# Two stacked graph-attention layers: the order of dense pieces, sums and transposes in the last stage

## The chip, the cores and the metric

The kernel runs on one core of a Trainium2 chip. The metric is the time of one execution on the device in microseconds. The kernel before took 2142.76 us, the median of three runs (2141.24 to 2143.43). Besides those there is one execution under the hardware profiler, which has a time of its own.

The engines named below are TensorE (PE in the profile; its weight loads are PEld), VectorE (DVE), ScalarE (ACT), GpSimd (POOL) and the synchronous engine that issues plain transfers (SP). SBUF is the on-chip memory, PSUM the accumulators that TensorE writes.

## The reference

There are 4096 nodes with 512 features each and one 0/1 adjacency matrix, sparse and densest at the low node numbers. `heads` is a graph-attention layer: the features are projected, each edge gets a leaky-ReLU score from its two ends, the scores of a node's edges go through a softmax, and the neighbours' projected rows are summed with these weights.

```python
x  = layernorm(x + heads(x, adj, W0, a0))                # layer 0: 8 heads of 64
h  = elu(heads(x, adj, W1, a1))                          # layer 1: 8 heads of 64
o  = elu(heads(h, adj, Wo, ao))                          # one head of 512
y  = relu(o @ lin1_w + lin1_b) @ lin2_w + lin2_b         # 512 -> 1024 -> 512
x  = layernorm(x + y)
```

All arithmetic is in float32. The change concerns the last three lines: the attention with one head of 512, the two dense layers behind it, and the residual and layernorm at the end.

## The kernel before, in words

**Stages.** The kernel first turns the adjacency into edge lists, with the projection for the first attention beside it; then come three attention stages. Each stage's projected rows lie in a table in device memory, from which the next one gathers. A last branch, for inputs whose lists would not fit, does not run here.

**Tiles, chunks, units.** The 4096 nodes are 32 tiles of 128. A tile's edges lie in chunks of 128, one edge to a partition. A unit is up to six chunks of one tile (`GC`); the last stage has 66 of them. Tiles 20 to 31 have one unit, tiles 5 to 19 two, tiles 1 to 4 three or four, and tile 0, the densest, has eleven in four parts.

**What a unit needs** (class `Attention`):
- `gather` (L1072): one indirect transfer for each chunk, issued by GpSimd, into one of four row buffers `g` (`GT`, so a buffer comes free when the sums of the unit four before are done).
- `spread` (L1085), once for each tile: small matmuls into `pss` put the destination's part of the score beside each edge; VectorE collects them (L1117, L1129). More than 20 chunks take several cuts, each collected before the next (L1121 to L1124).
- `weights` (L1135): three VectorE operations on the scores `z` (L1147 to L1150), and ScalarE's exponential `w` (L1158).
- `add` (L1160): VectorE makes weighted selection matrices `sm` from the node numbers and `w` (L1187), and TensorE multiplies them with the gathered rows into the tile's accumulator `acc` (L1212). These matmuls are called *sums* below.

**What a finished tile needs.** `inverse` (L1216) takes the reciprocal of the softmax's denominator, on VectorE. `fold` (L1437) divides (L1239, VectorE) and applies the ELU: two ScalarE operations (L1247, L1248) and one of VectorE (L1249). `turn` (L1442) transposes the result on TensorE (L1452) and lets ScalarE copy it from PSUM (L1453) into the block's buffer `sht`.

**Dense pieces.** Tiles come in nine blocks: 31, 30; then 29 to 26; then 1, 10, 11, 20; then 23, 0, 24, 25; then 2, 9, 12, 19; 3, 8, 13, 18; 4, 7, 14, 17; 5, 6, 15, 16; and 22, 21. When the last tile of a block is turned, the block's work for the two dense layers enters the list `ready` as pieces: as many of the first layer as the block has tiles (`first_dense`, L1468: matmuls L1475, ReLU by ScalarE L1478), then one of the second layer for each tile (`second_dense`, L1480). A second-layer piece loads the tile's residual row by SP (L1483), adds the bias to it on VectorE (L1484), and multiplies (L1487). Its epilogue stays in `open_` until `close` (L1464) is called: the sum with the residual (L1492), the layernorm (L1253 to L1266 on VectorE with two ScalarE operations, L1258 and L1259, between) and the store by SP (L1494). Residual rows have three buffers `xr`.

**What sets the order.** The stage is written under a manual schedule: every engine carries out its own instructions in the order in which the program issues them. The loop over the units (L1512 to L1533) is therefore the plan. A running number `due` grows by the unit's chunks times a `pace`, chosen so that a block's pieces are spread over the units of the next block; when it reaches one and `ready` isn't empty, a piece is issued. In the kernel before one pass of the loop issues, in this order: the score matmuls of a later tile; the transposes of the tile folded in the pass before; the weights of the next unit; the reciprocal of the tile just finished; the unit's `sm` and sums; a gather; the open epilogue; the fold of the tile just finished; the collection of the scores; and last the pieces that are due. After the loop come the last two turns and all the pieces that are left (L1534 to L1540).

Of the kernel before, what the change touches and what calls it, by code (L numbers as in the profile page):

```python
# [10 lines left out]
F32 = mybir.dt.float32  # L11
# [10 lines left out]
P = 128  # L22
N = 4096
F = 512
# [534 lines left out]
def sparse_path(  # L559
# [23 lines left out]
    nc = tc.nc  # L583
# [57 lines left out]
    x1_d = dram.tile([N, F], F32, name="sx1_d")  # L641
# [407 lines left out]
    def units_of(order):  # L1049
        units = []  # L1050
        for t in order:
            own = [
                Unit(t, [(p.first + i, n) for i, n in runs], slots)
                for p in pts if p.t == t for runs, *slots in p.units()
            ]
            own[0].first = own[-1].last = True
            units += own
        return units
# [186 lines left out]
    def elu(sb, o):  # L1245
        ex = sb.tile([P, F], F32, name="ex")
        nc.scalar.activation(ex, o, AF.Relu, scale=-1.0)  # L1247
        nc.scalar.activation(ex, ex, AF.Exp, scale=-1.0)  # L1248
        return lambda: nc.vector.scalar_tensor_tensor(o, ex, -1.0, o, op0=OP.add, op1=OP.max)  # L1249

    def layernorm(sb, y):
        bs = sb.tile([P, 6], F32, name="bs")
        nc.vector.bn_stats(bs, y)  # L1253
        mv = sb.tile([P, 2], F32, name="mv")
        nc.vector.bn_aggr(mv, bs)
        rs = sb.tile([P, 2], F32, name="rstd")
        lg, r = rs[:, 0:1], rs[:, 1:2]
        nc.scalar.activation(lg, mv[:, 1:2], AF.Ln, bias=eps)  # L1258
        nc.scalar.activation(r, lg, AF.Exp, scale=-0.5)  # L1259

        def rest():

            nc.vector.scalar_tensor_tensor(lg, mv[:, 1:2], EPS, r, op0=OP.add, op1=OP.mult)
            nc.vector.scalar_tensor_tensor(lg, lg, -0.5, r, op0=OP.mult, op1=OP.mult)
            nc.vector.scalar_tensor_tensor(r, lg, 1.5, r, op0=OP.add, op1=OP.mult)
            nc.vector.tensor_scalar(y, y, mv[:, 0:1], r, op0=OP.subtract, op1=OP.mult)  # L1266

        return rest
# [87 lines left out]
    with ExitStack() as pools:  # L1356
        big = pools.enter_context(tc.tile_pool(name="eb", bufs=1))
        sb = pools.enter_context(tc.tile_pool(name="es", bufs=2))
# [24 lines left out]
    sb = ctx.enter_context(tc.tile_pool(name="ls", bufs=2, reuse_waits="tile"))  # L1383
# [23 lines left out]
    with tc.tile_pool(name="tg", bufs=GT, side="right", reuse_waits="tile") as gp, \  # L1407
            tc.tile_pool(name="tb", bufs=1, side="right", reuse_waits="tile") as big, \
            tc.tile_pool(name="ta", bufs=2, space=PSUM, reuse_waits="tile") as pacc, \
            tc.tile_pool(name="tp", bufs=1, space=PSUM, reuse_waits="tile") as ps, tc.manual_schedule():  # L1410

        few = NT - 12
        blocks = [[NT - 1, NT - 2], [NT - 3 - i for i in range(NJ)]]
        blocks += [[1 + b, few // 2 - b, few // 2 + 1 + b, few - b] for b in range(few // NJ)]
        blocks.insert(3, [NT - 9, 0, NT - 8, NT - 7])
        blocks.append([NT - 10, NT - 11])
        assert sorted(sum(blocks, [])) == list(range(NT))
        order = [t for block in blocks for t in block]  # L1420
        units = units_of(order)
        at = Attention(st2, gp, wk, pacc, ps)
        for _ in range(GT):
            nc.gpsimd.memset(gp.tile([P, GC, F + HS], F32, name="g"), 0.0)
        for u in units[:GT]:
            at.gather(u)
        l1w = big.tile([P, FC, HID], F32, name="sl1w")
        nc.sync.dma_start(l1w, lin1_w.rearrange("(c p) o -> p c o", p=P))
        l2w = big.tile([P, HC, F], F32, name="sl2w")
        nc.sync.dma_start(l2w, lin2_w.rearrange("(c p) o -> p c o", p=P))  # L1430
        l1b_r = big.tile([HC, P], F32, name="sl1b_r")
        nc.sync.dma_start(l1b_r, lin1_b.rearrange("(c p) -> c p", p=P))
        l2b = big.tile([P, F], F32, name="sl2b")
        nc.sync.dma_start(l2b, lin2_b.partition_broadcast(P))
        hts, hids, ready, open_ = {}, {}, [], []

        def fold(t):  # L1437
            o = at.normal(sb, t)
            elu(sb, o)()
            return o  # L1440

        def turn(t, o):  # L1442
            b = next(b for b, block in enumerate(blocks) if t in block)
            j, nb = blocks[b].index(t), len(blocks[b])
            if j == 0:

                while any(r[1] == b - 2 and r[0] is first_dense for r in ready):
                    piece()
                hts[b] = big.tile([P, FC, NB], F32, name="sht", bufs=2)
            pt = ps.tile([P, FC, P], F32, name="pt")  # L1450
            for c in range(FC):
                nc.tensor.transpose(pt[:, c, :], o[:, ts(c, P)], ident)  # L1452
            nc.scalar.copy(hts[b][:, :, ts(j, P)], pt)  # L1453
            if j == nb - 1:
                per = HC // nb
                ready.extend((first_dense, b, range(i * per, (i + 1) * per)) for i in range(nb))
                ready.extend((second_dense, b, i) for i in range(nb))

        def piece():
            close()  # L1460
            of, *what = ready.pop(0)
            of(*what)

        def close():  # L1464
            while open_:
                open_.pop(0)()

        def first_dense(b, ks):  # L1468
            if 0 in ks:
                hids[b] = big.tile([P, HC, NB], F32, name="shid")  # L1470
            for k in ks:
                n = len(blocks[b]) * P
                p1 = ps.tile([P, NB], F32, name="p1", tag="p", bufs=2)[:, :n]
                for c in range(FC):
                    nc.tensor.matmul(  # L1475
                        p1, l1w[:, c, ts(k, P)], hts[b][:, c, :n], start=(c == 0), stop=(c == FC - 1)
                    )
                nc.scalar.activation(hids[b][:, k, :n], p1, AF.Relu, bias=l1b[:, k : k + 1])  # L1478

        def second_dense(b, j):  # L1480
            t = blocks[b][j]
            xr = sb.tile([P, F], F32, name="xr", bufs=3)
            nc.sync.dma_start(xr, x1_d[ts(t, P), :])  # L1483
            nc.vector.tensor_add(xr, xr, l2b)  # L1484
            p2 = ps.tile([P, F], F32, name="p2", tag="p", bufs=2)
            for k in range(HC):
                nc.tensor.matmul(  # L1487
                    p2, hids[b][:, k, ts(j, P)], l2w[:, k, :], start=(k == 0), stop=(k == HC - 1)
                )

            def rest():
                nc.vector.tensor_add(xr, p2, xr)  # L1492
                layernorm(sb, xr)()
                nc.sync.dma_start(out[ts(t, P), :], xr)  # L1494

            open_.append(rest)

        for t in order[:2]:
            at.spread(t)()
        at.weights(units[0])  # L1500
        l1b = big.tile([P, HC], F32, name="sl1b")
        pb = ps.tile([P, HC], F32, name="pt")
        nc.tensor.transpose(pb, l1b_r, ident[:HC, :HC])
        nc.vector.tensor_copy(l1b, pb)


        pace = {t: 0.0 for t in blocks[0]}
        for last, block in zip(blocks, blocks[1:]):
            chunks = sum(u.n for u in units if u.t in block)
            pace.update((t, 2 * len(last) / chunks) for t in block)  # L1510
        due, folded = 0.0, None
        for i, u in enumerate(units):  # L1512
            pos = order.index(u.t)
            spread = at.spread(order[pos + 2]) if u.first and pos + 2 < NT else None
            if folded:
                turn(*folded)
                folded = None
            if i + 1 < len(units):
                at.weights(units[i + 1])
            if u.first and pos > 0:  # L1520
                at.inverse(sb, order[pos - 1])
            at.add(u)
            if i + GT < len(units):
                at.gather(units[i + GT])
            close()
            if u.first and pos > 0:
                folded = order[pos - 1], fold(order[pos - 1])
            if spread:
                spread()
            due = min(due + u.n * pace[u.t], 2.5)  # L1530
            while due >= 1 and ready:
                due -= 1
                piece()  # L1533
        if folded:  # L1534
            turn(*folded)
        at.inverse(sb, order[-1])
        turn(order[-1], fold(order[-1]))
        while ready:
            piece()
        close()  # L1540
# [56 lines left out]
```

## Time and profile before

| what | us |
|---|---|
| median of three runs | 2142.76 |
| the profiled execution | 2328.89 |
| its span, first to last instruction | 2326.7 |
| the last stage in it | about 1550 to 2326.7 |
| busy in the span: TensorE / VectorE / GpSimd / ScalarE | 1776.6 / 1328.1 / 1161.8 / 658.9 |
| in 1550 to 2327, idle ahead of the transposes (L1452) | 29.0 |
| in 1550 to 2327, idle ahead of the sums (L1212) | 42.7 |
| in 1550 to 2327, idle of VectorE ahead of the bias on the residual row (L1484) | 65.3 |

In a line of the groups the columns are: source line, engine, operation, what it writes and reads, the shapes, how often; after the first bar the busy time in us and the mean of one in ns; after the second the time that the engine sat idle just before such instructions, and what ended it. A line of the timeline has start and duration in us, engine, line, operation, operands and count, and in brackets the idle time before it with its releaser. Matmuls of float32 are counted twice there: a dense piece is 16 or 32 of them. A wait that the profile ascribes to "issue" has no releaser that it can see. The span of the profiled execution is longer than the runs' median, so durations are taken from it and are added up against its own time.

### The profile page before, as it was taken

Reading aid. Unit: us, or ns where it says so; the run is one execution under the profiler, and the core shown is the slowest. Engines: PE = TensorE matmul, PEld = TensorE weight load, DVE = VectorE, ACT = ScalarE, POOL = GpSimd, SP = SyncE. Lnnn points to the kernel's source line nnn. Section 1 sums busy time; section 2 is a strip of 40 time slices with the busy share of each in tenths; the row PEclk is TensorE's granted clock in tenths of the full one; section 3 lists DMA queues with packets and bytes.
Section 4 is the critical chain, followed back from the end, with each engine's and each line's share of the span. In section 5 each row is a group of like instructions: output and inputs, shape, how many; then the busy total and the mean of one; then the engine's idle time right before and its main releaser. Section 6 shows DMA issues by size and latency. Waiting matters only on the chain.

```text
span 2326.7 us, 29282 instructions
## 1 busy us (share of the span) xinstructions
PE 1776.6 (76%) x8987; PEld 1038.4 (45%) x8987; DVE 1328.1 (57%) x3920; ACT 658.9 (28%) x2311; POOL 1161.8 (50%) x1662
## 2 busy tenths in 40 slices
PE   4778776643987775754997767746999898998997
PEld 3555442212665543531665444424445444444444
DVE  6887776744998776733777655733243424334322
ACT  3446776650332211100433221101111111121121
POOL 5424444456556664627556665646355634444300
PEclk9989997866999896875999988877999999999999
DMA  6434665525667775625566665545354524335301
GB/s 222 141 115 159 224 256 207 210 80 163 201 209 219 212 209 144 174 60 145 154 159 170 175 182 145 158 128 143 87 150 131 170 81 148 101 110 151 93 16 52
DMA packets 132589, 351.94 MB, mean 151 GB/s; under 512 B 41922, under 2 KB 42954, under 8 KB 128454
## 3 DMA queue, kind: packets, MB, share of 16 engines
q0 software_dynamic: 74160, 206.25, 33.1%
q1 hardware_dynamic: 58262, 143.72, 17.5%
q8 instruction: 74, 1.21, 0.2%
q14 instruction: 93, 0.76, 0.1%
HBM read 347.31 MB, written 42.24 MB: 167 GB/s over the span
## 4 chain that ended last, share of the span: by engine, by line
PE 36%; DVE 12%; issue 9%; another core or an unknown queue 6%; DMA 3%; POOL 3%; ACT 2%; SPq 0%; DVEq 0%; POOLq 0%; ACTq 0%
PE acc L1212 13%; PE p L1475 9%; PE ph L697 6%; PE p L1487 5%; DVE g L1200 4%; POOL g L1076 3%; DMA g<-table_t,idx 2%; DMA xr<-sx_d 1%; PE pt L683 1%; DVE bs L1253 1%; DVE sm L1179 1%; DVE sm L1187 1%; DVE xr L1492 1%; DVE z L1147 1%
## 5 line engine op out<-in xcount | busy, mean ns | idle before, releaser
L1076 POOL DMA_INDIRECT g<-table_t,idx x927 | 937.4, 1011 | 720.1 <-PE acc L1212 352.9
L1212 PE MATMUL acc<-g,sm 128*64 128x260 f32 (+2 forms) x4068 | 619.9, 424 | 219.9 <-DVE g L1200 100.7
L1212 PEld LDWEIGHTS acc<-g,sm 128*64 128x64 f32 x4068 | 347.9, 150 | 462.7 <-issue 177.8
L697 PE MATMUL ph<-sw_t,xt 128*128 128x264 f32 (+1 forms) x1536 | 408.4, 415 | 82.1 <-ACT xt L686 46.3
L697 PEld LDWEIGHTS ph<-sw_t,xt 128*128 128x128 f32 x1536 | 303.4, 204 | 154.2 <-ACT xt L686 63.0
L1200 DVE TENSOR_TENSOR g<-g,wp 128x2048 f32<-128x2048 f32 (+3 forms) x132 | 349.1, 2645 | 22.8 <-ACT wp L1155 20.2
L884 DVE MAX8 cand<-key 128x8 f32<-128x353 f32 (+55 forms) x467 | 197.3, 449 | 77.7 <-PE key L878 77.1
L1475 PE MATMUL p<-sht,sl1w 128*128 128x512 f32 (+1 forms) x576 | 229.3, 553 | 2.2 <-issue 1.2
L1487 PE MATMUL p<-sl2w,shid 128*128 128x512 f32 x512 | 227.0, 598 | 0.0
L686 ACT ACTIVATE xt<-pt 128x128 f32<-128x128 f32 x384 | 101.1, 278 | 286.5 <-PE pt L683 132.3
L710 ACT COPY hrow<-ph 128x260 f32<-128x260 f32 (+2 forms) x194 | 71.1, 373 | 311.1 <-PE ph L697 146.2
L1475 PEld LDWEIGHTS p<-sht,sl1w 128*128 128x128 f32 x576 | 107.6, 191 | 114.0 <-issue 108.7
L1487 PEld LDWEIGHTS p<-sl2w,shid 128*128 128x128 f32 x512 | 95.4, 190 | 120.1 <-issue 119.3
L1249 DVE SCALAR_TENSOR_TENSOR o<-ex,o 128x512 f32<-128x512 f32 x64 | 44.4, 694 | 182.8 <-ACT ex L1248 145.1
L877 PE MATMUL key<-sg,s_identb 128*128 128x512 bf16 (+1 forms) x258 | 111.6, 434 | 15.4 <-DVE cand L884 10.1
L848 ACT ACTIVATE sg<-raw 128x4096 bf16<-128x4096 int32 (+1 forms) x39 | 116.9, 2998 | 6.6 <-DMA raw<-in_adj_dram 3.7
L1478 ACT ACTIVATE shid<-p,sl1b 128x512 f32<-128x512 f32 (+1 forms) x72 | 46.0, 639 | 249.5 <-PE p L1475 212.0
L878 PE MATMUL key<-frac,places 128*128 128x512 bf16 (+1 forms) x258 | 111.1, 431 | 2.7 <-POOL places L784 2.7
L1187 DVE TENSOR_SCALAR sm<-iota_n,nl,w 128x64 f32<-128x64 f32 x339 | 83.1, 328 | 31.9 <-ACT w L1158 31.1
L1147 DVE TENSOR_TENSOR z<-s,g 128x16 f32<-128x16 f32 (+9 forms) x291 | 43.6, 174 | 92.0 <-DMA g<-table_t,idx 83.7
L1117 DVE TENSOR_REDUCE s<-pss 128x48 f32<-128x144 f32 (+21 forms) x108 | 32.1, 298 | 102.3 <-remote 55.1
L686 ACT ACTIVATION_READ_ACCUMULATOR xt<-pt 128x1 f32 x384 | 79.7, 208 | 0.0
(185 smaller groups left out, 1811.3 us busy)
## 6 DMA issues: line engine op xcount, KB each, us to landing
raw<-in_adj_dram SPq DMA_DIRECT2D x31, 2048.0 KB
table_t<-hrow SPq DMA_DIRECT2D x64, 260.0 KB
xr<-in_x_dram SPq DMA_DIRECT2D x64, 256.0 KB
g<-table_t,idx POOLq DMA_INDIRECT x927
table_t<-hrow SPq DMA_DIRECT2D x32, 257.0 KB
sx_d<-o SPq DMA_DIRECT2D x32, 256.0 KB
xr<-sx_d SPq DMA_DIRECT2D x32, 256.0 KB
out_dram<-xr SPq DMA_DIRECT2D x32, 256.0 KB
```

The lines of the kernel that those rows point to most:

```text
L686: nc.scalar.activation(xt[:, c, :], pt[:, c, :], AF.Copy, accum_out=st.xparts[:, c, t : t + 1])
L697: nc.tensor.matmul(ph[:n], columns(c), st.w[:, c, j], start=(c == 0), stop=(c == FC - 1))
L848: nc.scalar.activation(sg[:, ts(i, w)], raw[:, ts(i, w)], AF.Sign)
L877: nc.tensor.matmul(out_, ident_b, sg[:, j:e], start=True, stop=False)
L878: nc.tensor.matmul(out_, places[:, w], frac[:, j - w * KW : e - w * KW], start=False, stop=True)
L884: nc.vector.max(out=cand[:, at : at + 8], in_=part)
L1076: nc.gpsimd.indirect_dma_start(out=u.g[:, k, : self.st.row], out_offset=None, in_=self.st.table[:, :], in_offset=bass.IndirectOffsetOnAxis ...
L1187: nc.vector.tensor_scalar(sm[:, at + i], of_g, node[k], u.w[:, k], op0=OP.is_equal, op1=OP.mult)
L1200: nc.vector.tensor_mul(body, body, wp[:, :, :, None].to_broadcast(body.shape))
L1212: nc.tensor.matmul(out_[g * HN : (g + 1) * HN], sm[:, slot], rows(k), start=start, stop=stop)
L1475: nc.tensor.matmul(p1, l1w[:, c, ts(k, P)], hts[b][:, c, :n], start=(c == 0), stop=(c == FC - 1))
L1487: nc.tensor.matmul(p2, hids[b][:, k, ts(j, P)], l2w[:, k, :], start=(k == 0), stop=(k == HC - 1))
```

## The change

Five edits, all in the last stage.

- The list `ready` is looked at right after a pass has issued the score matmuls: `due` is counted up there, and one piece is issued if one is due, ahead of the weights, the `sm` and the sums of the unit. Pieces beyond it are issued where they were, at the end of the pass.
- The transposes of the tile folded in the pass before are issued behind the unit's sums and gather and ahead of the open epilogue. Before, they stood ahead of the weights and the sums.
- `due` is no longer counted up at the end of the pass.
- The load of a residual row is a function of its own, `rows_of`, which loads a row at most once.
- `piece` calls it for the piece next in the list, if that is one of the second layer, before it issues the piece at hand; `second_dense` finds its row loaded, or loads it.

```diff
-        hts, hids, ready, open_ = {}, {}, [], []
+        hts, hids, resid, ready, open_ = {}, {}, {}, [], []
...
         def piece():
             close()
             of, *what = ready.pop(0)
+
+            if ready and ready[0][0] is second_dense:
+                rows_of(*ready[0][1:])
             of(*what)
+
+        def rows_of(b, j):
+            t = blocks[b][j]
+            if t not in resid:
+                resid[t] = sb.tile([P, F], F32, name="xr", bufs=3)
+                nc.sync.dma_start(resid[t], x1_d[ts(t, P), :])
...
         def second_dense(b, j):
             t = blocks[b][j]
-            xr = sb.tile([P, F], F32, name="xr", bufs=3)
-            nc.sync.dma_start(xr, x1_d[ts(t, P), :])
+            rows_of(b, j)
+            xr = resid.pop(t)
             nc.vector.tensor_add(xr, xr, l2b)
...
             spread = at.spread(order[pos + 2]) if u.first and pos + 2 < NT else None
-            if folded:
-                turn(*folded)
-                folded = None
+            due = min(due + u.n * pace[u.t], 2.5)
+            if due >= 1 and ready:
+
+                due -= 1
+                piece()
             if i + 1 < len(units):
                 at.weights(units[i + 1])
...
             if i + GT < len(units):
                 at.gather(units[i + GT])
+            if folded:
+                turn(*folded)
+                folded = None
             close()
...
             if spread:
                 spread()
-            due = min(due + u.n * pace[u.t], 2.5)
             while due >= 1 and ready:
```

## The prediction, made before the changed kernel was run

> **What bounds the kernel now.** I read first the page, to see which engine carries the span. All busy shares are averages over four stages, so I then took the groups of instructions of the last stage alone (1550 us to the end), because the change touches nothing before it:
>
> ```profile
> L1475 PE MATMUL p<-sht,sl1w 128*128 128x512 f32 (+1 forms) x576 | 229.3, 553 | 2.2 <-issue 1.2 <-DVE xr L1492 1.0
> L1487 PE MATMUL p<-sl2w,shid 128*128 128x512 f32 x512 | 227.0, 598 | 0.0
> L1212 PE MATMUL acc<-g,sm 128*64 128x257 f32 (+1 forms) x1356 | 204.7, 421 | 42.7 <-DMA g<-table_t,idx 23.2 <-DVE rd L1224 10.3 <-DVE sm L1187 4.8
> ...
> L1452 PE MATMUL pt<-s_ident,o 128*128 128x128 f32 x128 | 23.0, 310 | 29.0 <-DVE o L1249 16.2 <-issue 12.8
> ...
> L1484 DVE TENSOR_TENSOR xr<-xr,sl2b 128x512 f32<-128x512 f32 x32 | 22.1, 691 | 65.3 <-DMA xr<-sx_d 60.3 <-issue 5.0
> ```
>
> TensorE is busy for 680 of 777 us: the stage is its own work plus its gaps. So an edit pays only by closing a gap. The largest are 23.2 us at the start for the first gathers, which stay, and 29.0 us ahead of the transposes. VectorE loses 60.3 us on the residual rows, but VectorE has room. The third view is the timeline at a place where the transposes wait (tile 25 ends the fourth block, tile 2 begins the fifth):
>
> ```profile
> 1852.08 7.13 PE L1487 MATMUL p<-sl2w,shid 128*128 128x512 f32 x16
> ...
> 1859.75 3.13 PE L1212 MATMUL acc<-g,sm 128*64 128x257 f32 x24
> ...
> 1860.36 0.70 DVE L1492 TENSOR_TENSOR xr<-p,xr 128x512 f32<-128x512 f32 x1
> ...
> 1863.64 0.75 DVE L1239 TENSOR_SCALAR o<-acc,rd 128x512 f32<-128x512 f32 x1
> ...
> 1865.74 0.73 DVE L1249 SCALAR_TENSOR_TENSOR o<-ex,o 128x512 f32<-128x512 f32 x1 [1.36 <-ACT ex L1248]
> ...
> 1866.53 1.12 PE L1452 MATMUL pt<-s_ident,o 128*128 128x128 f32 x4 [3.65 <-DVE o L1249]
> ...
> 1867.26 1.42 DVE L1187 TENSOR_SCALAR sm<-iota_n,nl,w 128x64 f32<-128x64 f32 x6
> 1867.62 5.27 PE L1212 MATMUL acc<-g,sm 128*64 128x257 f32 x24
> ```
>
> Two things are to be seen. VectorE works in one order: end of the dense piece's epilogue, then the fold (L1239 to L1249), and only then the sm of the next unit (L1187). And the sums after the gap take 5.27 us where 24 of them elsewhere take 2.82.
>
> The last view is the timeline of TensorE where tile 20 ends the third block, the shape that matters most below:
>
> ```profile
> 1744.31 7.13 PE L1487 MATMUL p<-sl2w,shid 128*128 128x512 f32 x16
> ...
> 1751.39 0.63 PE L1452 MATMUL pt<-s_ident,o 128*128 128x128 f32 x4
> 1751.95 2.82 PE L1212 MATMUL acc<-g,sm 128*64 128x257 f32 x24
> 1754.70 7.13 PE L1475 MATMUL p<-sht,sl1w 128*128 128x512 f32 x16
> ```
>
> No gap at all: a dense piece of 7.1 us runs while VectorE folds and makes the next sm.
>
> [...]here 24 sums cost 5.27 against 2.82 us after 3.65 us idle, and 16 cost 3.77 against 1.95 after 2.42[...]. [...]the residual load at 1949.10 lets its add start at 1954.13, the last one at 2312.62 at 2316.39, so 3.8 to 5.0 us here.
>
> **The change, part by part.** I wrote out the loop's two orders through the 66 units; the old one gives the trace's order exactly. "Piece" is 7.1 us of TensorE, "sums" 1.95 (16 matmuls) or 2.82 us (24).
>
> *Order.* Old: sums(i), piece, transposes of the tile folded in i, sums(i+1). New: piece, sums(i), transposes of the tile folded in i-1, close, fold. In the steady state this is a rotation: between two sums there is still one piece. VectorE's chain there is epilogue 3.4 (1711.26 to 1714.63), fold 2.8, then sm, and fits: after a piece's end the next sm is ready at 8.1 us, the next sums are due at 9.0. Cost nothing; the piece is the cover.
>
> What moves is which sums have no piece ahead when no piece is due or the list is empty. Then these sums wait for VectorE. From the end T of a second-layer piece, an epilogue with a fold behind it puts the next sums at T + 3.35 + 3.98 (fold start 1863.64 to sums 1867.62) = T+7.3. Where the new order has transposes ahead of the epilogue, ScalarE's copy of them (L1453) is ahead of the layernorm's Ln, and the Ln starts 1.17 us after the transposes start (1859.18 to 1860.34), instead of T+1.75: 2.2 us more after sums of 24, 1.35 after 16. So T+9.7. A dense piece right behind the transposes waits 1.26 us for the copy, which the old order hid under sums.
>
> *Losses.* T is always the end of the second-layer piece that empties the list, and the same work is counted in both orders. (1) End of the third block, tile 20: old two times 3.4 us of sums and transposes (1751.28 to 1754.70, and as much ahead of the piece) = 6.8 to the next first-layer piece, no gap. New: sums of tile 23 and transposes of tile 11 to T+3.4; first sums of tile 0 only at T+9.7[...]; transposes of tile 20, copy, piece at T+16.3. Loss 9.5. (2) End of the fourth block, tiles 24 and 25: old 13.8 (1859.05 to 1872.82) + 3.4 = 17.2. New: sums of tile 25 to 3.4, first sums of tile 2 from 9.7 to 15.0, transposes of tile 24, copy to 16.2; the fold of tile 25 has its Relu behind that copy, so tile 2's next sums start at 19.5 and end cold at 24.8, piece at T+26.0. Loss 8.8. (3) Tile 11, whose second unit has no piece due: new sums at T+7.4 instead of T+2: 5.4 idle and about 2.5 cold; the old order's waits behind tile 0's four score cuts, about 2.2, go. Loss 5.7. (4) Tiles 22, 21 before the end: old 11.0 + 2.6 = 13.6; new sums of tile 22 at T+5.8, cold to 11.1, those of 21 behind its reciprocal at 11.95 to 16.2, piece at 17.5. Loss 3.9. (5) Start: the copy ahead of the first dense piece is bare, 1. Sum 28.9.
>
> *Gains.* (a) Tile 12's first unit, which folds and has no piece due: old 4.26 + 0.53 idle and 1.7 cold; new idle 3.4 ahead of one sums, then the piece: 14.7 to 12.4, gain 2.3. (b) Block ends with two units in the last tile (19, 18, 17): the epilogue is not held by a late residual add. Old, from the last piece but one to the next first-layer piece, less 7.0 for the piece between: 1943.27 to 1967.63, 17.4; 2032.58 to 2053.71, 14.1; 2118.48 to 2143.50, 18.0. New: sums at T+5.8 behind the epilogue, the next at 10.4 behind the fold, their transposes and the copy: 14.1, and 15.8 with sums of 24. Gain 3.3 + 0 + 2.2 = 5.5. (c) Tile 0, whose units have no folds: 2.42 and 3.42 idle with 1.8 and 3.1 cold shrink; worked out 5.8, but GpSimd issues 45 gathers of 1.3 us here, so I take 5. (d) Residual rows a piece sooner. The loads no longer stand on the synchronous queue between the store just issued and the add. Most of the 60.3 us is under a piece and worth nothing; without that cover it would all be lost. What dense runs lose of TensorE outside the places counted is 1.7 (sums of 16 that took 2.40, 2.33, 2.17 and 2.38 for 1.95 us, and a gap of 0.26). At the very end it counts in full: the last second-layer piece ends at 2315.63,
>
> ```profile
> 2312.62 0.38 SPq L1483 DMA_DIRECT2D xr<-sx_d  x1
> 2316.39 0.69 DVE L1484 TENSOR_TENSOR xr<-xr,sl2b 128x512 f32<-128x512 f32 x1 [4.22 <-DMA xr<-sx_d]
> 2317.18 0.69 DVE L1492 TENSOR_TENSOR xr<-p,xr 128x512 f32<-128x512 f32 x1
> ```
>
> and its add to 2317.18 starts at 2315.73: 1.45, with the 0.99 bare wait at 2289.40: 2.4. A load now passes one store on that queue; the third row buffer exists already, and the store that frees it was issued a piece before, so no new wait. GpSimd's gathers keep their place behind the sums that free their buffers. Sum 16.9.
>
> *Not shown by the trace:* how cold the sums run when the gap is 6 us. [...]I take 2.5 each, seen after 3.65 us.
>
> **Sum.** 28.9 - 16.9 = +12.0 us in the profiled execution (2328.89 us, span 2326.7). It runs 186 us above the median of 2142.76, but the last stage shows full clock outside its gaps, so I carry the difference over unscaled: 2142.8 + 12.0 = 2154.8 us. A change of 0.2% (4.3 us) is about what a measurement here tells from none.
>
> **Rivals.** *Half the loss* (0.18): if the sums after the long gaps restart warm and epilogue and fold overlap better than added up, losses are half, 14.5 - 16.9 = -2.4: 2140, no change. For it: gaps under 1.5 us cost no clock in this trace. Against: in-order VectorE leaves no overlap. *Faster* (0.12): the folds of tiles 20, 24, 10 and 16 are ready before the piece ends, so no sums wait and only the gains stay: 2143 - 17 = 2126. For it: VectorE gets 60.3 us of load waits back. Place: L1187 of tile 0's first unit. It decides if L1239 of tile 20 starts before the piece of tile 26 ends; in the order written, the epilogue L1492 stands ahead of it and waits for that end, so I think not. If the transposes' full 26 us (29.0 less the last, 2.7) went with nothing in their place, it would be 2117. *No gains in the middle* (0.08): tile 0 stays bound by its gathers and the residual loads were hidden anyway; only the tail's 2.4 is left of the gains: 2143 + 26 = 2169.
>
> **How the numbers follow.** Likeliest (0.62): 2154.8, its own range 2147 to 2163. Range for 8 in 10: the likeliest and the first rival, 2138 to 2166. Slower 0.62 + 0.08 = 0.70, same 0.18, faster 0.12.
>
> **What would show it.** Right: waits of L1452 nearly gone (the last 2.7 us stays), but waits of L1212 for sm up from 4.8 to 30 us or more, with gaps of about 6 us ahead of the first sums of tiles 0 and 2 and the second of tile 11; the wait of L1484 for its load near zero; the layernorm's Ln behind L1453. Wrong: if the first sums of tile 0 follow within 2 us of the transposes of tile 11, or if TensorE's idle time in the stage falls.

## The result and the profile after

The changed kernel takes 2176.23 us, the median of four runs (2175.3 to 2176.79), against 2142.95 for the kernel before: a ratio of 1.0156 [1.0139, 1.0174], or 33.3 us more. The prediction was 2154.8, 12.0 us more, in a range of 2138 to 2166. The direction was right; the size was not.

The profiled execution of before that the prediction was made from took 2328.89 us, 186 more than the timed runs. Two of the chips used below take nearly as long for this same kernel (2333.75 and 2319.0 us); which chip that profile came from is not on record. So a second profile of before was taken on a chip where its median is 2142.95 us (E0 below, 2146.28 us, span 2144.0), and the profile after (span 2174.5) is set against that one.

From the last clearing of a gather buffer to the end of the span, the last stage takes 751.3 us in E0 and 787.2 after: 35.9 more. Everything ahead of it takes 1392.7 and 1387.3; in E1 to E3 below, which have the same code there, it takes 1384.9 to 1391.2, so these 5.4 us are no effect of the change. The loss lies in the last stage, all of it.

First the groups of instructions of the last stage, after (columns as in the prediction: line, engine, operation, operands, count; busy us and mean ns; idle time just before, and what ended it):

```profile
L1484 PE MATMUL p<-sht,sl1w 128*128 128x512 f32 (+1 forms) x576 | 225.1, 548 | 5.4 <-ACT sht L1453 5.4
L1212 PE MATMUL acc<-g,sm 128*64 128x256 f32 (+1 forms) x1356 | 207.8, 432 | 65.6 <-DVE sm L1187 41.3 <-DMA g<-table_t,idx 23.7 <-PE acc L1212 0.5
...
L1493 DVE TENSOR_TENSOR xr<-xr,sl2b 128x512 f32<-128x512 f32 x32 | 21.9, 683 | 3.2 <-DMA xr<-sx_d 3.2
...
L1452 PE MATMUL pt<-s_ident,o 128*128 128x128 f32 x128 | 20.9, 286 | 2.7 <-DVE o L1249 2.7
...
L1101 PE MATMUL pss<-hole,s_identb 128*128 128x18 bf16 (+11 forms) x33 | 6.0, 181 | 23.4 <-DVE s L1117 23.4
```

And the same groups of the kernel before, in E0 (there the bias on the residual row is L1484):

```profile
L1475 PE MATMUL p<-sht,sl1w 128*128 128x512 f32 (+1 forms) x576 | 228.7, 553 | 0.8 <-DVE xr L1492 0.8
L1212 PE MATMUL acc<-g,sm 128*64 128x257 f32 (+1 forms) x1356 | 198.2, 409 | 40.1 <-DMA g<-table_t,idx 21.9 <-DVE sm L1187 17.8
...
L1484 DVE TENSOR_TENSOR xr<-xr,sl2b 128x512 f32<-128x512 f32 x32 | 22.1, 691 | 67.3 <-DMA xr<-sx_d 67.3
...
L1452 PE MATMUL pt<-s_ident,o 128*128 128x128 f32 x128 | 21.6, 295 | 28.8 <-DVE o L1249 28.8
...
L1101 PE MATMUL pss<-hole,s_identb 128*128 128x18 bf16 (+11 forms) x33 | 5.9, 178 | 2.0 <-DVE s L1117 2.0
```

The change does what it says: the transposes' 28.8 us of waiting are 2.7, and VectorE's 67.3 us for the residual rows are 3.2. In their place the sums wait 41.3 us for `sm` instead of 17.8 and run 9.6 us longer; the clock granted to TensorE is 0.93 of full speed over the stage after, and over the whole span 0.910, for 0.916 in E0. The dense matmuls wait 5.4 us for ScalarE's copy, where they didn't. Those three the prediction had named. The last line it had not: the small score matmuls of `spread` (L1101) wait 23.4 us for VectorE instead of 2.0.

Where the time went, by the first dense piece of each block (us added from E0 to after in each stretch, beside the sum of the prediction's terms that fall in it, with the 1.7 us of (d) spread over its places):

| stretch | measured | predicted |
|---|---|---|
| start to first block | +5.1 | +1.0 |
| to the second | +6.2 | 0 |
| to the third (tiles 11, 20) | +15.9 | +14.5 |
| to the fourth (tiles 0, 24, 25) | +14.5 | +3.8 |
| to the fifth (tiles 2, 9, 12, 19) | -4.4 | -5.6 |
| to the sixth, the seventh | +1.4, -2.6 | -0.4, -2.4 |
| to the eighth, and from there to the end | +4.1, -4.3 | +3.5, -2.4 |
| sum | +35.9 | +12.0 |

From the fourth block's first piece on, the forecast is within 2 us at every step. Of the 23.9 us that it lacks, 22.4 are in the first four rows.

The end of the third block shows both kinds of loss. The timeline after (start, duration; in brackets the idle time before, with its releaser):

```profile
1576.11 0.19 DVE L1117 TENSOR_REDUCE s<-pss 128x13 f32<-128x39 f32 x1
...
1576.36 0.20 PE L1101 MATMUL pss<-hole,s_identb 128*128 128x18 bf16 x1 [2.65 <-DVE s L1117]
...
1576.48 8.50 PE L1496 MATMUL p<-sl2w,shid 128*128 128x512 f32 x16
...
1584.91 2.82 PE L1212 MATMUL acc<-g,sm 128*64 128x257 f32 x24
...
1588.36 0.58 ACT L1453 COPY sht<-pt 128x512 f32<-128x512 f32 x1 [10.36 <-PE pt L1452]
1588.84 0.30 ACT L1258 ACTIVATE rstd<-mv,s_eps 128x1 f32<-128x1 f32 x1
...
1593.16 0.17 DVE L1117 TENSOR_REDUCE s<-pss 128x6 f32<-128x18 f32 x1
...
1593.39 0.20 PE L1101 MATMUL pss<-hole,s_identb 128*128 128x18 bf16 x1 [5.07 <-DVE s L1117]
...
1594.56 5.71 PE L1212 MATMUL acc<-g,sm 128*64 128x257 f32 x24 [0.90 <-DVE sm L1187]
...
1601.53 1.98 PE L1484 MATMUL p<-sht,sl1w 128*128 128x512 f32 x4 [0.68 <-ACT sht L1453]
```

And the same place in E0:

```profile
1576.33 0.17 PE L1101 MATMUL pss<-hole,s_identb 128*128 128x18 bf16 x1
...
1576.43 0.64 PE L1452 MATMUL pt<-s_ident,o 128*128 128x128 f32 x4
...
1577.00 2.82 PE L1212 MATMUL acc<-g,sm 128*64 128x257 f32 x24
...
1579.75 7.13 PE L1475 MATMUL p<-sht,sl1w 128*128 128x512 f32 x16
```

From the end of the second-layer piece (T = 1584.98) the first sums of tile 0 start at T + 9.6 and the next dense piece at T + 16.5; the prediction had 9.7 and 16.3. The first three lines are what it didn't have. A dense piece is due and could run, but the score matmul stands ahead of it on TensorE, and that waits until VectorE has collected the scores of the tile before (L1117 at 1576.11). The piece then runs 8.50 us instead of 7.13, at a granted clock of 0.83. In E0 the score matmul comes right behind a piece and waits for nothing.

### The profile page after: what moved, and what is told of

The parts are those of the page before. It is cut to its first block, busy times and chain, and to the rows that moved or that the text cites. A ratio compares the mean times of both kernels' runs of the same rounds, so it can differ in the third digit from the quotient of the medians.

```text
span 2174.5 us, 29275 instructions
## 1 busy us (share of the span) xinstructions
PE 1729.2 (80%) x8987; PEld 1019.2 (47%) x8987; DVE 1323.7 (61%) x3920; ACT 663.2 (30%) x2311; POOL 1165.3 (54%) x1662
## 4 chain that ended last, share of the span: by engine, by line
PE 36%; DVE 13%; issue 8%; DMA 7%; POOL 6%; ACT 2%; POOLq 0%; DVEq 0%; ACTq 0%; SPq 0%
PE acc L1212 11%; PE p L1496 10%; PE p L1484 10%; DMA g<-table_t,idx 7%; POOL g L1076 6%; DVE g L1200 5%; PE ph L697 3%; DVE sm L1179 1%; PE pt L1452 1%; DVE o L1232 1%; DVE z L1147 1%; DVE z L1150 1%; DVE z L1148 1%; DVE bs L1253 1%; ACT sht L1453 1%
## 5 line engine op out<-in xcount | busy, mean ns | idle before, releaser
L1212 PE MATMUL acc<-g,sm 128*64 128x260 f32 (+2 forms) x4068 | 590.7, 424 | 223.7 <-DVE g L1200 152.9
L697 PE MATMUL ph<-sw_t,xt 128*128 128x264 f32 (+1 forms) x1536 | 396.6, 407 | 45.8 <-ACT xt L686 39.0
L697 PEld LDWEIGHTS ph<-sw_t,xt 128*128 128x128 f32 x1536 | 295.4, 199 | 113.0 <-ACT xt L686 58.3
L1496 PE MATMUL p<-sl2w,shid 128*128 128x512 f32 x512 | 231.4, 607 | 0.0
L1484 PE MATMUL p<-sht,sl1w 128*128 128x512 f32 (+1 forms) x576 | 225.1, 548 | 5.4 <-ACT sht L1453 5.4
L1484 PEld LDWEIGHTS p<-sht,sl1w 128*128 128x128 f32 x576 | 107.9, 190 | 111.3 <-issue 100.9
L1501 DVE TENSOR_TENSOR xr<-p,xr 128x512 f32<-128x512 f32 x32 | 22.1, 691 | 133.7 <-PE p L1496 133.7
L1155 ACT ACTIVATE wp<-z 128x32 f32<-128x32 f32 (+3 forms) x132 | 27.2, 206 | 206.5 <-DVE g L1200 206.2
```

The costliest lines, as they stand in the source:

```text
L697: nc.tensor.matmul(ph[:n], columns(c), st.w[:, c, j], start=(c == 0), stop=(c == FC - 1))
L1212: nc.tensor.matmul(out_[g * HN : (g + 1) * HN], sm[:, slot], rows(k), start=start, stop=stop)
L1484: nc.tensor.matmul(p1, l1w[:, c, ts(k, P)], hts[b][:, c, :n], start=(c == 0), stop=(c == FC - 1))
L1496: nc.tensor.matmul(p2, hids[b][:, k, ts(j, P)], l2w[:, k, :], start=(k == 0), stop=(k == HC - 1))
```

## The experiments

Each was run against the kernel before on its own chip: E0 to E3 on one chip, E4 to E7 on another, E8 to E11 on a third. On the last two the kernel before takes 2333.75 and 2319.0 us. Where an expectation names a time near 2143, its difference to that is what to compare. E1 to E3 each do one part alone, E4 and E5 two parts.

**E0, the kernel before, unchanged.**

> The kernel before, unchanged, profiled once more: the first profiled execution of it took 2328.89 us against a median of 2142.76, so its gaps may not be those of the timed runs. In the trace of the changed kernel the last stage (from the last clearing of a gather buffer to the end of the span) takes 787 us after 1387 us of other stages. If the whole 33 us are in the last stage, this trace has 1387 us ahead of it and about 754 in it. Rival, the earlier stages were moved too: about 1370 ahead of it and 773 in it, as in the first trace.

2146.28 us, one execution, with 1392.7 us ahead of the last stage and 751.3 in it, as first expected. Against the first profile the last stage is 21.7 us shorter (751.3 for 773.0) and what lies ahead of it 161.0. The 21.7 are 14.0 up to the second block's first piece, 6.6 on the way from the third block to the fourth, where tile 0 lies, and 1.1 elsewhere. So not all gaps that term (c), tile 0, was read off are in the timed runs: of the two there (2.42 and 3.42 us), E0 has one, of 2.37 us.

**E1, residual rows a piece sooner, alone** (`rows_of` and `second_dense` as in the change; the order of the loop as before).

```diff
         def piece():
             close()
             of, *what = ready.pop(0)
+            if ready and ready[0][0] is second_dense:
+                rows_of(*ready[0][1:])
             of(*what)
```

> Only the residual rows a piece sooner. My theory: the wait of the bias add for its load (60 us of VectorE) goes to nearly nothing and is worth 1.45 + 0.99 us at the end and one or two more inside, so 2139 to 2141. Rival, the early load is what costs (a store held behind it, or traffic beside the gathers): 2150 or more.

2127.85 us, ratio 0.9921 [0.9907, 0.9936]: 15 us faster. The transposes wait as before (27.0 us in 8 places for 28.8), but the sums wait 11.4 us for `sm` instead of 17.8. A late row load had held VectorE (67.3 us idle ahead of the bias in E0), and with it the next `sm`, which stands behind that bias. This part is a gain, well above the 2 to 4 us expected. In the last stage it is 12 us: 6.7 between the fourth block's first piece and the seventh's, where term (b) had 5.5 for rows that come in time, 2.6 behind the last block's first piece, and 4.5 on the way to the second and third blocks; some 2 us are lost elsewhere.

**E2, transposes behind the sums, alone.**

```diff
-            if folded:
-                turn(*folded)
-                folded = None
             if i + 1 < len(units):
                 at.weights(units[i + 1])
...
                 at.gather(units[i + GT])
+            if folded:
+                turn(*folded)
+                folded = None
             close()
```

> Only the transposes behind the next unit's sums; pieces stay behind the sums and the score matmuls are covered as before. My theory: the transposes' own move costs little, the copy bare ahead of a block's first piece (8 times 0.7) and the epilogue's Ln behind it at tiles of one unit, 5 to 10 us: 2148 to 2153. Rival, the moved transposes and the ScalarE copy in front of the epilogue are the main cost: 2165 or more.

2179.31 us, 1.0162 [1.0145, 1.018]: 36 us slower, more than the whole change, and where the rival had it. The sums wait 82.3 us for `sm` in 28 places (20.9 of that is the first gather, which E0's trace puts down to the transfer). One such place, in the timeline of E2 (SPq is SP's queue of transfers):

```profile
1552.47 0.18 DVE L1255 BATCH_NORM_AGGREGATE mv<-bs 128x2 f32<-128x6 f32 x1
...
1555.84 0.59 ACT L1453 COPY sht<-pt 128x512 f32<-128x512 f32 x1 [5.83 <-PE pt L1452]
1556.33 0.30 ACT L1258 ACTIVATE rstd<-mv,s_eps 128x1 f32<-128x1 f32 x1
...
1558.05 0.34 SPq L1494 DMA_DIRECT2D out_dram<-xr  x1
...
1558.48 0.38 SPq L1483 DMA_DIRECT2D xr<-sx_d  x1
```

The layernorm's statistics are ready at 1552.65, but its Ln starts 3.7 us later. ScalarE has the copy of the transposes first in its queue, and the copy waits for transposes that now stand behind the sums. The normalised row, its store and the next residual load, which is issued after that store, are all as much later, and the load's bias addition is ahead of the next `sm` on VectorE.

**E3, the due piece in front, alone** (transposes behind that piece and ahead of the sums; rows loaded late).

```diff
             spread = at.spread(order[pos + 2]) if u.first and pos + 2 < NT else None
+            due = min(due + u.n * pace[u.t], 2.5)
+            if due >= 1 and ready:
+                due -= 1
+                piece()
             if folded:
                 turn(*folded)
                 folded = None
...
             if spread:
                 spread()
-            due = min(due + u.n * pace[u.t], 2.5)
```

> Only the due piece in front of the sums; the transposes stay ahead of the sums, behind that piece, and the residual rows are loaded late. My theory: sums lose their cover at block ends and at tile 11, and the score matmuls, now ahead of the piece, wait for VectorE to have collected the scores before them (26 us of waits in the trace of the changed kernel): 2155 to 2165. Rival, the transposes are the main cost: within 5 us of 2143.

2149.33 us, 1.0031 [1.0018, 1.0043]: 6 us slower, between the two expectations. The piece in front costs 11.6 us on the way to the third block and 4.1 on the way to the fourth, and gives 8.5 back on the way to the fifth. So this part alone makes losses of the predicted kind, and its gains cover most of them. The score matmuls wait with a due piece behind them here too, ahead of the third block and of the fourth:

```profile
1558.59 0.20 PE L1101 MATMUL pss<-hole,s_identb 128*128 128x18 bf16 x1 [2.66 <-DVE s L1117]
...
1670.74 0.19 PE L1101 MATMUL pss<-hole,s_identb 128*128 128x27 bf16 x1 [3.53 <-DVE s L1117]
```

The three parts alone add up to -15 + 36 + 6 = +27, and together they measure +33; E5 below shows that they still aren't independent.

**E4, rows and front** (the whole change without moving the transposes), and **E5, rows and transposes** (without the piece in front). The edits are those of E1 and E3, and of E1 and E2.

> The whole change without the move of the transposes: they stay ahead of the weights and the sums, behind the due piece. If the parts add up (rows alone -15, piece in front alone +6): 2134, faster than before, and the transposes' move is what makes the change slow. Rival, my first theory, that the sums lose their cover by the piece's move: 2150 or more even with the rows early.

> Rows a piece sooner and the transposes behind the sums; pieces stay behind the sums. If the parts add up (-15 and +36): 2164. If most of what the transposes cost alone was the late load behind a late store (epilogue late, so store late, so the next row late), the early rows take that away: 2150 or less.

E4: 2327.7 against 2333.75, 0.9982 [0.997, 0.9995], 6 us faster. E5: 2339.65, 1.0029 [1.0012, 1.0046], 6 us slower. The transposes' move is what turns a small gain into the loss: without it the rest of the change is a little faster than before. And early rows take most of the harm out of the transposes when no piece is in front: +6 in E5, where the parts alone would add up to +21. That fits a loss in E2 that ran for the most part through the late row. The harm returns when a piece is put in front as well; the next five look into that combination.

**E6, ScalarE's copy behind the layernorm.** The whole change, with the transposes issued after `close` and the fold. TensorE's order stays the same, and only the copy is no longer ahead of Ln, and of the next fold's Relu, on ScalarE.

```diff
-            if folded:
-                turn(*folded)
-                folded = None
             close()
-            if u.first and pos > 0:
-                folded = order[pos - 1], fold(order[pos - 1])
+            new = (order[pos - 1], fold(order[pos - 1])) if u.first and pos > 0 else None
+            if folded:
+                turn(*folded)
+            folded = new
```

> The changed kernel with the transposes issued one step later, behind the epilogue and the fold. TensorE's order is the same to the instruction; only ScalarE's is not: its copy of the transposes no longer stands ahead of the layernorm's Ln and the next fold's Relu. Theory that this copy is the cost: 2150 to 2162. Rival, that TensorE's order (sums without cover, score matmuls in front) is the cost: within 5 us of 2176.

2355.97, 1.0095 [1.007, 1.0121]: still 22 us slower than before, which lies between the two expectations (7 to 19, or 28 to 38), against 31 for the change itself on another chip of that kind (E8). In the last stage it is 791.4 us for E8's 801.6. By this the copy's place is about a third of the loss. That comparison crosses chips; E10 repeats it on one.

**E7, rows sooner and the fold ahead of the open epilogue**, in the old order otherwise.

```diff
-            close()
             if u.first and pos > 0:
                 folded = order[pos - 1], fold(order[pos - 1])
+            close()
```

> The kernel before with the rows a piece sooner and the fold of the finished tile ahead of the open epilogue, so that it runs under the dense piece and not behind its end. Theory that what TensorE waits for at block ends is the fold behind the epilogue: the 27 us of waits of the transposes go but for the last 2.7, the sums wait about 1 us behind the epilogue in their place, cold starts go too: 2095 to 2110. Rival, the wait only moves to the sums: 2120 to 2128.

2305.11 against 2333.75, 0.9876 [0.9848, 0.9903]: 28.6 us faster than the kernel before, the largest gain of all, and between the two expectations (33 to 48, or 15 to 23). Early rows alone gave 15 us on E1's chip. What the transposes had waited for was a fold queued behind an epilogue that TensorE's next work doesn't need. TensorE in E7 at the end of the fourth block, the place of the prediction's third view:

```profile
1867.73 2.82 PE L1212 MATMUL acc<-g,sm 128*64 128x257 f32 x24
1870.49 0.66 PE L1452 MATMUL pt<-s_ident,o 128*128 128x128 f32 x4
1874.86 5.17 PE L1212 MATMUL acc<-g,sm 128*64 128x257 f32 x24 [3.71 <-DVE sm L1187]
```

The transposes follow the sums at once, where they waited 3.65 us. Here the wait only moves to the next sums, since VectorE has the epilogue to do in any case: the next piece comes at T + 12.9 instead of 13.8. Over the stage the transposes' waits fall to 2.7 us.

**E8, the changed kernel again, and E9, score matmuls behind the due piece.** E9 changes one thing in the changed kernel:

```diff
-            spread = at.spread(order[pos + 2]) if u.first and pos + 2 < NT else None
             due = min(due + u.n * pace[u.t], 2.5)
             if due >= 1 and ready:
                 due -= 1
                 piece()
+            spread = at.spread(order[pos + 2]) if u.first and pos + 2 < NT else None
```

> The changed kernel again, beside the three below on one chip[...]. As against the kernel before: +25 to +35 us.

> The changed kernel with the score matmuls of a later tile behind the due piece, not ahead of it. They have one accumulator, and in the trace of the changed kernel they wait 26 us for VectorE to have emptied it, with the dense piece queued behind them on TensorE. Theory that this is what my sum left out: 12 to 18 us less than the changed kernel. Rival, the same time is then waited ahead of the sums: within 5 us of it.

E8: 2350.35 against 2319.0, 1.0141 [1.0099, 1.0182], so the change's loss is there on this chip too (+31). E9: 2343.15, 1.0096 [1.0065, 1.0127]. E9 is 7 us below E8 in the medians, and 10.0 in the last stage (791.6 for 801.6): the suspected wait is real, at somewhat less than the expected 12 to 18. TensorE at one place of the second block, first in E8:

```profile
1622.67 0.66 PE L1452 MATMUL pt<-s_ident,o 128*128 128x128 f32 x4
1625.98 0.18 PE L1101 MATMUL pss<-hole,s_identb 128*128 128x27 bf16 x1 [2.66 <-DVE s L1117]
...
1626.14 8.66 PE L1496 MATMUL p<-sl2w,shid 128*128 128x512 f32 x16
```

and then in E9:

```profile
1631.22 0.66 PE L1452 MATMUL pt<-s_ident,o 128*128 128x128 f32 x4
1631.71 7.03 PE L1496 MATMUL p<-sl2w,shid 128*128 128x512 f32 x16
1638.58 0.18 PE L1101 MATMUL pss<-hole,s_identb 128*128 128x24 bf16 x1
```

From transposes to piece it is 3.47 us in E8 and 0.49 in E9, and the piece is 1.6 us shorter. Not all of the wait goes: in the whole stage the score matmuls still wait 19.7 us for VectorE (30.1 in E8), nearly all of it at places where no piece was due to cover them.

**E10, E9 with the copy behind the layernorm, and E11, E9 with the fold first.** E10 adds E6's edit to E9. E11 does instead:

```diff
+            new = (order[pos - 1], fold(order[pos - 1])) if u.first and pos > 0 else None
             if folded:
                 turn(*folded)
-                folded = None
+            folded = new
             close()
-            if u.first and pos > 0:
-                folded = order[pos - 1], fold(order[pos - 1])
```

> As the one before, with the transposes issued behind the epilogue and the fold, so that ScalarE's copy no longer stands ahead of Ln and Relu. If that copy is the transposes' cost: 15 us or more less than the one before. If it is that the sums, and with them the transposes and the next block's first piece, come behind epilogue and fold: within 8 us of it, since the copy then stands behind the fold and the first piece of a block waits for it.

> The changed kernel with the score matmuls behind the piece, and the fold of the finished tile ahead of the transposes and of the epilogue: the fold then runs under the dense piece instead of behind its end. If the fold queued behind the epilogue is what makes uncovered sums late: 20 to 30 us less than the run with the score matmuls moved, so 10 us or more faster than the kernel before. If not: within 10 us of that run.

E10: 2325.42, 1.004 [1.0023, 1.0056]. E11: 2322.82, 1.001 [0.9991, 1.003]. In the medians E10 is 17.7 us below E9 and E11 20.3. But E9 has six runs, which lie up to 15 us apart, and its profiled one is 6 us below their median. In the last stage of the profiles, one of each, the times are 801.6 (E8), 791.6 (E9), 782.4 (E10), 777.9 (E11): 10.0 us for the score matmuls' wait, 9.2 for E10's edit to E9 and 13.7 for E11's. So E10's 15 us or more are met by the medians and not by the profiles, and the copy's place is worth something between 9 and 18 us. E11 keeps the change's idea, piece first and transposes behind the sums. With its two orders changed it gains on E9 what was expected by the medians, and less by the profiles, and it only comes level with the kernel before and not 10 us below it, although it has E1's early rows, which gave 15 us alone on E1's chip. If they are worth as much on this chip, the new order itself still costs about what the rows bring. Part of that is the sums with no piece ahead of them: in E9 and E10 alike the second sums of tile 11 wait 5.45 us for their `sm` and then run 4.6 and 4.9 us instead of 2.8.

## Why the prediction was wrong in size

**What failed is the step *Order*: "Cost nothing; the piece is the cover".** It followed VectorE's chain as far as the next `sm`, and checked that against the sums. It left out that each pass issues score matmuls of a later tile first, and that these have one accumulator, `pss`, which they can't fill again until VectorE has collected what is in it. That collection stands behind epilogue and fold on VectorE, some 6.1 us after the end of a piece (1570.02 to 1576.11 in the trace after), while TensorE has sums for only 3.7 of them. In the old order a piece lay between; in the new one the piece that should be the cover is queued behind the waiting matmul. In the trace after no due piece passes the waiting score matmul: at the three places counted next the piece starts 0.15, 0.12 and 0.16 us after the score matmul.

What this costs can be added up after at the three places where a due piece stands behind such a wait: 2.66 us, and 1.68 for the slower piece, ahead of the second block; 2.65 and 1.37 ahead of the third; 3.65, and 1.68 for a piece of 8.81 us, ahead of the fourth. That is 13.7 us, none of which E0 has. Three more waits, of 2.68 us and twice 5.07, hold nothing, since the sums behind them wait another 0.9 us for `sm` anyway. On its chip E9 gave 10.0 us of this kind back; a part of the wait then falls ahead of sums instead.

Two of the three places are in E3 as well, so they come with the piece in front. The one ahead of the second block is in none of E2 to E5: it comes only with the piece in front and the transposes behind the sums together. There the collection comes late for another reason, which is ScalarE's queue (after):

```profile
1456.15 0.58 ACT L1453 COPY sht<-pt 128x512 f32<-128x512 f32 x1 [2.77 <-PE pt L1452]
1456.63 0.63 ACT L1247 ACTIVATE ex<-o 128x512 f32<-128x512 f32 x1
...
1457.95 0.69 DVE L1249 SCALAR_TENSOR_TENSOR o<-ex,o 128x512 f32<-128x512 f32 x1 [9.73 <-ACT ex L1248]
...
1458.57 0.15 DVE L1117 TENSOR_REDUCE s<-pss 128x1 f32<-128x3 f32 x1
...
1458.77 0.17 PE L1101 MATMUL pss<-hole,s_identb 128*128 128x27 bf16 x1 [2.66 <-DVE s L1117]
```

The copy of the transposes stands ahead of the fold's Relu (L1247), so VectorE sits idle until the fold's exponential is done, and the collection is behind that.

**Term (5), the start, was mis-sized.** It had 1 us for a bare copy; the start measured 5.1. E2 has 4.9 there and E3 none, so it is the transposes' move:

```profile
1427.09 0.59 ACT L1453 COPY sht<-pt 128x512 f32<-128x512 f32 x1 [6.16 <-PE pt L1452]
1427.57 0.63 ACT L1247 ACTIVATE ex<-o 128x512 f32<-128x512 f32 x1
...
1430.90 5.62 PE L1212 MATMUL acc<-g,sm 128*64 128x257 f32 x24 [0.92 <-DVE sm L1187]
```

Here too the copy holds the fold's Relu. The sums of the fourth tile come 1.7 us later than in E0 and run 5.62 us for 3.48 (granted clock 0.55 after), and then 1.3 us of transposes and copy are bare ahead of the first piece.

**Term (c), tile 0, was read off another execution, and the rest of it didn't come.** Of its two gaps E0 has one (first line), and after the change that gap is still there, now for a gather (second line):

```profile
1641.48 4.07 PE L1212 MATMUL acc<-g,sm 128*64 128x257 f32 x16 [2.37 <-DVE sm L1187]
...
1672.52 0.65 PE L1212 MATMUL acc<-g,sm 128*64 128x257 f32 x2 [2.27 <-DMA g<-table_t,idx]
```

From what else changed on the way to the fourth block, tile 0 gained about 2 us of the 5, an estimate: 5.3 for the score matmuls and 11.1 for loss (2) are 16.4, and 14.5 were measured.

**The losses (1) to (4)** were right in place and in mechanism, though two of the sizes were not. The sums of tile 2 come at T + 9.6 and T + 19.9 (predicted 9.7 and 19.5) and the piece behind them at T + 27.1 (26.0); the second sums of tile 11 at T + 7.4 (7.4); the eighth block's first piece, loss (4), at T + 17.7 (17.5). Against E0, loss (2) is 11.1 us for 8.8, since the old order takes 16.0 there and not 17.2; loss (3) is 2.8 for 5.7, since E0's sums at that place are already late and slow (5.76 us for 3.69 behind tile 0's score cuts). The copy ahead of Ln was in these terms at 2.2 us a place; that it also stands ahead of the next fold's Relu was in (2) alone. The slower sums behind the gaps were priced at 2.5 us in each place and measured 2.9 and 3.2 (5.71 and 5.99 for 2.82, at a granted clock of 0.54 and 0.52), and 2.0 at tile 11 (4.77, at 0.65). The end of the second block, which the sum left out, lost 1.9 us beside the score matmuls' wait: its next sums wait 6.20 us for `sm`. Together 13.7, 4.1 of (5), 3 of (c), 1.9, 2.3 of (2) and -2.9 of (3) make 22.1 of the 22.4 us that the first four rows lacked.

**The gains (a), (b) and (d).** From the fourth block's first piece to the end they came out nearly as predicted, with loss (4) among them: -5.8 measured for -7.3. Block ends measured 14.4, 15.7 and 15.3 us for the predicted 14.1, 14.1 and 15.8; tile 12, 10.2 for 12.4. The tail came as told:

```profile
2161.42 0.68 DVE L1493 TENSOR_TENSOR xr<-xr,sl2b 128x512 f32<-128x512 f32 x1
...
2165.01 0.69 DVE L1501 TENSOR_TENSOR xr<-p,xr 128x512 f32<-128x512 f32 x1 [2.91 <-PE p L1496]
```

The bias is on the row 2.9 us before the last addition, which starts within 0.1 us of the piece's end. In the old order (b) and (d) were too small together: alone, early rows give 15 us, 12 of them in the last stage, and the terms have 9.6. How much of the rest is left in the changed kernel no run shows.

**The rivals.** *Half the loss* and *faster* fall: tile 20's fold (L1239) starts 5.5 us after the piece's end, at 1590.47, and the sums after the long gaps ran slow. *No gains in the middle* (2169) is the nearest number, for a reason that is mostly wrong: tile 0 does stay bound by a gather, but the middle's other gains came, and the loss was larger.

**What stays open.** How the 36 us of E2 divide between copy, late loads and uncovered sums on the chip of the timed runs: E4 to E11 ran on slower chips, and their steps are carried over as sizes, not as exact shares. And why transposes that cost 6 us more than before beside early rows (E5) cost more once a piece is in front. The score matmuls' wait ahead of the second block, which needs both, is 4.3 us of it; for the rest no run isolates a cause.

## What to carry to other kernels

Before a piece of long work is moved to the front as cover, list everything that the same engine has ahead of it in the new order, and ask of each, however small, which single buffer it must wait for and where the release stands in the other engine's queue. A move on one engine moves its partner on the next: transposes put behind the sums took their ScalarE copy ahead of a layernorm, whose Ln at one place in E2 came 3.7 us late, and so delayed a store, a load and the next `sm`. When an instruction waits on a queue, look first at what stands ahead of the work that releases it: taking the fold ahead of an epilogue that TensorE didn't need, with loads a piece sooner, gained 28.6 us on its chip, where the reordering lost 31 to 33 on two others.

## What the runs showed of the hardware

- The same kernel took 2142.95 us on one chip, 2319.0 on a second and 2333.75 on a third. Away from the gaps a dense piece of 16 matmuls took 7.03 to 7.13 us on all of them, with a granted clock of 1.00 (the pieces at 1744.31 in the first profile of before, 1562.97 after). Between the two profiles of before, 161.0 of 182.7 us lie ahead of the last stage, and the gaps of tile 0 differ, so a gap read off one execution needn't be there in another. The cause of the difference was not found.
- In the changed kernel a dense piece behind 2.65 to 3.65 us of idle TensorE ran 8.5 to 8.8 us instead of 7.1, at a granted clock of 0.81 to 0.83, and 24 sums behind 3.7 to 6.2 us ran 4.8 to 6.0 instead of 2.8, at 0.65 to 0.52. In the first profile of before 24 sums behind a gap of 3.65 us and the transposes ran 5.27 us, at 0.59, and 16 sums behind 2.42 us ran 3.77 instead of 1.95, at 0.61. In E2 24 sums behind 2.05 us ran 5.17. The length alone doesn't tell: behind waits of 2.65 and 2.66 us ahead of the third block the piece took 7.11 us in E4 and in E8.
- Sums behind a short gap took longer at full clock, too. In the first profile of before 24 sums behind 0.84 us of idle TensorE took 3.48 us instead of 2.82, and 16 sums behind 1.46 us took 2.40 instead of 1.95, both at a granted clock of 1.00. In E0 24 sums behind 0.82 us took 3.48 us.
